# Fixed slots for a batch-wise attention stage of a four-part transformer block, with four smaller moves around it

## The chip, the cores and the metric

The kernel runs on one core of one Trainium2 chip. The metric is the device time of one execution in microseconds (us); lower is better. The core has five engines that each take their own instructions in order and wait for one another through semaphores: TensorE (PE) does matrix products and transposes, VectorE (DVE) and ScalarE (ACT) do element-wise work, GpSimd (POOL) does a few small operations and indexed transfers, and SyncE (SP) issues the other transfers between the memory of the chip (DRAM) and the core's own memory. Matrix products are accumulated in a small memory of their own (PSUM) and have to be copied out of it by DVE or ACT.

## The reference, cut to what matters

Tokens are 8 batches of 512 with 256 features, all in 32-bit floats. Four sublayers follow each other; each adds its output, times a learned scalar, to the tokens:

```python
x = x + tanh(g_xattn[0]) * gated_cross_attention(layernorm(x), ctx, boxes)   # 16 heads of 64, keys from ctx
x = x + tanh(g_ffn[0])   * ffn0(layernorm(x))
x = x + tanh(g_xattn[1]) * cross_attention(layernorm(x), ctx)                # one head of 256, then Wl on 8 copies
x = x + tanh(g_ffn[1])   * spiking_ffn(layernorm(x))                         # relu^2, then 5 steps of a neuron
```

Inside `ffn0` the attention runs across the batch, not along the sequence, and a mixture of experts with a hard capacity follows:

```python
y1 = ln(x + mha(x))             # 4 heads of 64; the 8 tokens with the same position attend to each other
gates = softmax(y1 @ wg); idx = argmax(gates)          # 8 experts
loc = number of earlier tokens with the same idx       # in the order of position, then batch
keep = loc < 512                                       # the others get nothing
y2 = ln(y1 + keep * gate * expert[idx](y1))            # 256 -> 1024 -> 256
```

The last sublayer ends in five steps per element, each with a comparison, a multiply-add and a reset:

```python
mem = 0.9 * mem + y - (mem > 1);  spikes += (mem > 1)
```

## The kernel before, in words

The kernel has five stages, one after the other.

1. `gated_cross_attention`, lines 258 to 584. A prologue goes over the 8 batches (lines 366 to 382). For each it loads the context and the tokens (`load`), makes keys, values and queries with 512-column products and stores them to DRAM (lines 221, 237 and 250), and makes small box terms (`box`, lines 137 to 158). Between batches it also loads constants for the gates (`wst`, twice 928 KB), the output weights `wo` and the box keys `kd`, and it prepares the first gate features: `offsets` on DVE, `sizes` and `log` on ACT, then `turns`, `whole`, `rest` and `rest_sizes` on DVE, `sines` on ACT, and `place`, four transfers of 520 KB. Key and query results go through a staging tile `st` with four buffers. In the prologue the order on every engine is made by the framework's scheduler. The main loop over 32 query tiles (lines 535 to 584) is written out by hand for PE, ACT and DVE and is not changed.
2. `batch_attention`, lines 591 to 763. The 4096 tokens form 32 tiles of 128 tokens (16 positions by 8 batches), in 8 groups of four. `project(g)` normalises a group, transposes it, and makes queries and keys (four 512-column pairs, `pq`) and values (`pv`). `attend(j)` takes one tile: scores for four heads (`pS`), a mask that leaves only tokens of the same position (`sm`), the row maximum (`nm`), four exponentials (`e`), their transposes (`pT`, copied to `eT` by ACT), the products with the values (`po`, scaled to `o` by DVE), two transposes (`pt2`, copied to `oT` by ACT), the output product (`pw`) and the residual (`res`). `finish(g)` normalises the group (`y1`), stores it, transposes it and makes the logits `lg`. The scheduler orders all engines. After each group `late.load(g)` fetches weights for later stages; at group 2 it also sums the 8 blocks of the matrix `WlT` into `wl` on DVE, from a staging tile with one buffer, in two loads of 1024 KB.
3. `experts`, lines 988 to 1070. `late.keys(b)` makes keys and values of the third sublayer for all 8 batches; `route` (lines 766 to 860) turns the logits into a slot for every token, a chain of small DVE steps with three products in its middle; 32 indexed transfers on POOL scatter the tokens (line 1000); then eight experts run, each on 512 tokens.
4. and 5. `tail`, lines 1076 to 1413, gathers the experts' results and does sublayers three and four for one batch after the other, in an order written by hand. Its last lines (1392 to 1413) run the two last batches: `hidden` and `drive` are products, `neurons(b, t0, t1)` is a chain of 13 DVE operations on the tiles t0 to t1 of a batch, read from `y`, which ACT copies out of PSUM.

A pool hands its memory on when it is closed, and the first instruction that writes memory of a closed pool waits for the last user of it, a store by a transfer included. In `with tc.manual_schedule(engines=...)` the engines named keep the program's own order.

Of the kernel before, what the change touches and what calls it, by code (L numbers as in the profile page):

```python
# [11 lines left out]
F32 = mybir.dt.float32  # L12
# [7 lines left out]
P = 128  # L20
# [4 lines left out]
LH = 4  # L25
# [232 lines left out]
def gated_cross_attention(cx, a, tg, x1d, d):  # L258
# [4 lines left out]
    with ExitStack() as es:  # L263
# [90 lines left out]
        with ExitStack() as pro:  # L354
            batch = project_all(cx, a, d, pro)
            bp = pro.enter_context(tc.tile_pool(name="bq", bufs=1))
            box = box_terms(cx, a, d, pro)
            bx = bp.tile([P, NSTEP * NP, 2], F32, name="bx")
            nc.sync.dma_start(out=bx, in_=a["boxq"])
            nc.sync.dma_start(out=crow, in_=a["crow"])  # L360
            nc.vector.tensor_tensor(qs, bx[:, :, 0], bx[:, :, 1], ALU.add)
            nc.vector.tensor_scalar(qs, qs, 0.5, None, ALU.mult)
            nc.vector.tensor_tensor(qi, bx[:, :, 1], bx[:, :, 0], ALU.subtract)
            nc.vector.tensor_scalar(qi, qi, 1.0, None, ALU.add)
            nc.vector.reciprocal(qi, qi)
            for b in range(B):
                batch(b)
                box(b)
                if b == 0:
                    for w in wst:  # L370
                        nc.sync.dma_start(out=w[0:GR], in_=a["wst"])
                    nc.sync.dma_start(out=wo, in_=a["woT"])
                    bo = cx.bcast(cp, a["bo"], "bo")
                    load_keys(0)
                if b in (1, 3, 5):
                    j = b // 2
                    offsets(j, 0, NP)
                    features(j, sizes, clip, log)
                if b in (2, 4):
                    j = b // 2 - 1  # L380
                    load_products(j)
                    features(j, turns, whole, rest, rest_sizes, sines, place)
# [208 lines left out]
def batch_attention(cx, a, y1, lg, x1d, y1d, between):  # L591
# [4 lines left out]
    with ExitStack() as es:  # L596
# [25 lines left out]
        yg_ = y1d.rearrange("(l g s) d -> g s l d", l=B, s=P // B)  # L622

        def load(g):
            xg = wk.tile([P, 4, D], F32, name="xg", tag="xg")
            for j in range(4):
                nc.sync.dma_start(out=xg[:, j, :], in_=xg_[4 * g + j])
            return xg

        def project(xg):  # L630
            mv, rs = cx.stats(wk, xg, 4)
            xf = wk.tile([P, 4, D], F32, name="xf", tag="xf")
            cx.normalize(xf, xg, mv, rs, 4)
            xfT = wk.tile([P, 2, 4 * P], F32, name="xfT", tag="xfT")
            for c in range(2):
                pt = ps.tile([P, 4, P], F32, name="pt", tag="t", bufs=2)
                for j in range(4):
                    nc.tensor.transpose(pt[:, j, :], xf[:, j, c * P : (c + 1) * P], ident)
                nc.scalar.copy(xfT[:, c, :], pt.rearrange("p j t -> p (j t)"))
            qkT = wk.tile([P, 4, 4 * P], F32, name="qkT", tag="qkT")  # L640
            for m in range(4):
                pq = ps.tile([P, 4 * P], F32, name="pq", tag="q", bufs=2)
                for c in range(2):
                    nc.tensor.matmul(
                        pq, wi[:, c, m * P : (m + 1) * P], xfT[:, c, :],
                        start=(c == 0), stop=(c == 1),
                    )
                nc.scalar.activation(qkT[:, m, :], pq, AF.Identity, bias=bqk[:, m : m + 1])
            v = wk.tile([P, 4, D], F32, name="v", tag="v")
            for j in range(0, 4, 2):  # L650
                pv = ps.tile([P, 2, D], F32, name="pv", tag="q", bufs=2)
                for k in range(2):
                    for c in range(2):
                        nc.tensor.matmul(
                            pv[:, k, :], xfT[:, c, (j + k) * P : (j + k + 1) * P],
# [3 lines left out]
                    v[:, j : j + 2, :], pv, bv.unsqueeze(1).to_broadcast([P, 2, D]), ALU.add  # L659
                )  # L660

            nc.vector.tensor_tensor(xf, xf, ob.unsqueeze(1).to_broadcast([P, 4, D]), ALU.add)
            return xf, qkT, v

        def attend(j, xf, qkT, v, res):

            tok = slice(j * P, (j + 1) * P)
# [15 lines left out]
            e = wk.tile([P, LH, P], F32, name="e", tag="e")  # L683
            se = wk.tile([P, LH], F32, name="se", tag="se")
            for k in range(LH):
                nc.scalar.activation(
                    e[:, k, :], smf[:, k, :], AF.Exp, bias=nm[:, k : k + 1],
                    accum_out=se[:, k : k + 1],
                )
            rec = wk.tile([P, LH], F32, name="rec", tag="rec")  # L690
            nc.vector.reciprocal(rec, se)
            pT = ps.tile([P, LH, P], F32, name="pT", tag="t", bufs=2)
            for k in range(LH):
                nc.tensor.transpose(pT[:, k, :], e[:, k, :], ident)
            eT = wk.tile([P, LH, P], F32, name="eT", tag="eT")
            nc.scalar.copy(eT, pT)
            po = ps.tile([P, LH, HD], F32, name="po", tag="o")
            for k in range(LH):
                h = 2 * (k % 2) + k // 2
                nc.tensor.matmul(  # L700
                    po[:, h, :], eT[:, k, :], v[:, j, h * HD : (h + 1) * HD],
                    start=True, stop=True,
                )
            o = wk.tile([P, LH, HD], F32, name="o", tag="o")
# [5 lines left out]
            )  # L710
            pt = ps.tile([P, 2, P], F32, name="pt2", tag="t", bufs=2)
            of = o.rearrange("p h d -> p (h d)")
            for c in range(2):
                nc.tensor.transpose(pt[:, c, :], of[:, c * P : (c + 1) * P], ident)
            oT = wk.tile([P, 2, P], F32, name="oT", tag="oT")
            nc.scalar.copy(oT, pt)
# [3 lines left out]
            nc.vector.tensor_tensor(res[:, j, :], pw, xf[:, j, :], ALU.add)  # L720

        def finish(g, res):
            mv, rs = cx.stats(wk, res, 4)
            for j in range(4):
                y = y1[:, 4 * g + j, :]
                nc.vector.scalar_tensor_tensor(
                    y, res[:, j, :], mv[:, j, 0:1], g1, ALU.subtract, ALU.mult
                )
                nc.vector.scalar_tensor_tensor(y, y, rs[:, j : j + 1], b1, ALU.mult, ALU.add)
                nc.sync.dma_start(out=yg_[4 * g + j], in_=y)  # L730
            pl = ps.tile([P, 4, NE], F32, name="pl", tag="l")
            for j in range(0, 4, 2):
                pt = ps.tile([P, 2, 2, P], F32, name="pt3", tag="t", bufs=2)
                for k in range(2):
                    for c in range(2):
                        nc.tensor.transpose(
                            pt[:, k, c, :], y1[:, 4 * g + j + k, c * P : (c + 1) * P], ident
                        )
                yT = wk.tile([P, 2, 2, P], F32, name="yT", tag="yT")
                nc.scalar.copy(yT, pt)  # L740
                for k in range(2):
                    for c in range(2):
                        nc.tensor.matmul(
                            pl[:, j + k, :], yT[:, k, c, :], wg[:, c, :],
                            start=(c == 0), stop=(c == 1),
                        )
            nc.vector.tensor_copy(lg[:, 4 * g : 4 * g + 4, :], pl)

        xgs = {0: load(0)}
        nxt = project(xgs.pop(0))  # L750
        last = None
        for g in range(NG):
            cur = nxt
            if g + 1 < NG:
                nxt = project(load(g + 1))
            res = wk.tile([P, 4, D], F32, name="res", tag="res")
            for j in range(4):
                attend(j, *cur, res)
            if last is not None:
                finish(g - 1, last)  # L760
            last = res
            between(g)
        finish(NG - 1, last)


# [110 lines left out]
class Late:  # L876
# [43 lines left out]
    def load(self, g):  # L920
# [14 lines left out]
        if g == 2:  # L935

            self.w["wl"] = wl = pool.tile([P, 2, D], F32, name="wl")
            with tc.tile_pool(name="wl8", bufs=1) as w8:
                for c in range(2):
                    wl8 = w8.tile([P, 8, D], F32, name="wl8", tag="wl8")  # L940
                    nc.sync.dma_start(out=wl8, in_=a["WlT"][:, :, c, :])
                    nc.vector.tensor_reduce(
                        wl[:, c, :], wl8.rearrange("p j d -> p d j"), AX.X, ALU.add
# [10 lines left out]
    def open(self, es):  # L954
        tc = self.cx.tc
        self.wk = es.enter_context(tc.tile_pool(name="kwk", bufs=2))
        self.ps = es.enter_context(tc.tile_pool(name="kps", bufs=2, space=PSUM))

    def keys(self, b):
        nc, w, d, wk, ps = self.cx.nc, self.w, self.d, self.wk, self.ps  # L960
        ctxT = self.ctxT.pop(b)
        for m in range(2):
            pp = ps.tile([P, S], F32, name="pp", tag="p")
# [5 lines left out]
            kT = wk.tile([P, S], F32, name="kT", tag="kT", bufs=3)  # L969
            nc.scalar.activation(kT, pp, AF.Identity, bias=w["bk"][:, m : m + 1])  # L970
            nc.sync.dma_start(out=d["ck"][b][:, m, :], in_=kT)
        for k in range(0, NQ, 2):
            pv = ps.tile([P, 2, D], F32, name="pv", tag="p")
# [6 lines left out]
            v = wk.tile([P, 2, D], F32, name="v", tag="v", bufs=3)  # L980
# [4 lines left out]
        self.context(b + self.AHEAD)  # L985


def experts(cx, a, y1, lg, late, moe, gkd, disp, yd, between):

    tc, nc, ident = cx.tc, cx.nc, cx.ident  # L990
    with ExitStack() as es:
        late.open(es)
        late.keys(0)
# [31 lines left out]
        for b in range(1, B):  # L1025
            late.keys(b)
# [49 lines left out]
def tail(cx, d, w, cp, x1, y1d, gslot, gk, yd, tg, out):  # L1076
# [5 lines left out]
    with ExitStack() as es:  # L1082
# [271 lines left out]
        with tc.manual_schedule(engines=TAIL_MANUAL):  # L1354
# [47 lines left out]
            features(("e", f + 1))  # L1402
            drive(f, 2, 2)
            drive(f, 3, 3)
            fire = neurons(f)
# [11 lines left out]
def flamingo_gated_block(ctx: ExitStack, tc: tile.TileContext, a, out):  # L1417
# [32 lines left out]
    with ExitStack() as es:  # L1450
# [12 lines left out]
        batch_attention(cx, a, y1, lg, x1d, y1d, late.load)  # L1463
# [142 lines left out]
```

## Time and profile before

| | us |
|---|---|
| median of 3 runs | 3078.8 |
| lowest and highest run | 3076.96 and 3089.75 |
| the profiled execution, its own time | 3057.43 |
| its span (first to last instruction) | 3055.6 |
| prologue (first instruction to the first gate product) | 0 to 373.4 |
| batch attention (first load of tokens to the last logits) | 1981.2 to 2279.9 |
| route and scatter (to the first expert's transposes) | 2279.9 to 2346.4 |
| experts (to the last gathers) | 2346.4 to 2584.5 |
| tail | 2584.5 to 3055.6 |

Busy time of the engines in the span: PE 2927.1 us (96%), its weight loads 2128.4, DVE 1818.9 (60%), ACT 1406.5 (46%), POOL 138.2. In rows of the profile a line such as `pw<-ow,oT 128*128 128x256 f32 x4` names the result, its inputs, the shape and how many instructions were merged; 32-bit products appear as two records each. The ends of matrix products are modelled, so a busy PE can hold gaps that only the starts of the instructions show. `[idle before <-releaser]` says how long an engine stood idle and what ended it.

### The profile page before, as it was taken

The page shows a single profiled execution, that of the slowest core. Times are in us where ns is not written, and L with a number is a line of the kernel's source. Part 1 is how long each engine was busy: PE and PEld are TensorE (multiplying, and loading weights), DVE is VectorE, ACT ScalarE, POOL GpSimd, SP SyncE. Part 2 cuts the span into 40 slices and gives each one's busy share as a digit, 9 for nine tenths or more (in the row PEclk, how much of TensorE's full clock was granted, in tenths as well). Part 3 has the DMA queues.
Part 4 walks back from the last instruction along what each step waited for, and adds up shares of the span by engine and source line. Part 5 has one row for each costly group of instructions (what it writes and reads, how often), then busy time and mean ns, then how long its engine had stood idle before and what let it go on. Part 6 is the DMA issues. An engine that isn't in the chain of part 4 may idle for free. (4 is left out here: it accounts for less than half of the span.)

```text
span 3055.6 us, 39493 instructions
## 1 busy us (share of the span) xinstructions
PE 2927.1 (96%) x15334; PEld 2128.4 (70%) x15334; DVE 1818.9 (60%) x2828; ACT 1406.5 (46%) x2196; POOL 138.2 (5%) x130
## 2 busy tenths in 40 slices
PE   7999999999999999999999999889999997799998
PEld 3444478888888888888888888756665665456566
DVE  2532276777777777777777766565542101666757
ACT  2532256656566556665656564234431111243433
POOL 1000000000000000000000000000004000221100
PEclk9999999999999999999999999999979999899999
DMA  6766565464555555555545554440016332111100
GB/s 221 223 186 189 157 193 164 130 167 132 165 135 159 139 157 142 149 157 141 156 137 156 137 161 123 119 171 28 22 49 213 134 117 105 62 42 59 32 14 21
DMA packets 275099, 394.47 MB, mean 129 GB/s; under 512 B 55456, under 2 KB 139056, under 8 KB 271736
## 3 DMA queue, kind: packets, MB, share of 16 engines
q1 hardware_dynamic: 271840, 383.54, 43.3%
q0 software_dynamic: 3072, 8.39, 0.8%
q8 instruction: 122, 2.00, 0.3%
q14 instruction: 65, 0.53, 0.1%
HBM read 237.24 MB, written 86.46 MB: 106 GB/s over the span
## 5 line engine op out<-in xcount | busy, mean ns | idle before, releaser
L451 ACT ACTIVATE e<-pS,nm 128x512 f32<-128x512 f32 x512 | 323.7, 683 | 576.4 <-DVE nm L448 576.0
L424 PE MATMUL pg<-wst,emb 116*128 116x208 f32 (+1 forms) x2560 | 581.4, 350 | 6.7 <-DVE gate L430 5.6
L424 PEld LDWEIGHTS pg<-wst,emb 116*128 116x128 f32 x2560 | 414.0, 189 | 203.2 <-issue 80.6
L480 PEld LDWEIGHTS po<-v,at 128*128 128x128 f32 x4096 | 493.0, 192 | 0.1
L480 PE MATMUL po<-v,at 128*128 128x65 f32 x4096 | 485.7, 272 | 0.0
L448 DVE TENSOR_REDUCE nm<-pS 128x2 f32<-128x1024 f32 x256 | 312.5, 1221 | 180.5 <-PE pS L444 179.3
L462 DVE SCALAR_TENSOR_TENSOR at<-gate,pT 128x1024 f32<-128x1024 f32 x256 | 311.0, 1215 | 46.7 <-PE pT L460 45.6
L444 PE MATMUL pS<-kT,qT 64*128 64x512 f32 x1024 | 291.3, 641 | 6.6 <-DMA kT<-kdr 2.9
L460 PE MATMUL pT<-ident,e 128*128 128x128 f32 x2048 | 266.4, 273 | 0.0
L460 PEld LDWEIGHTS pT<-ident,e 128*128 128x128 f32 x2048 | 239.7, 141 | 14.0 <-issue 2.3
L430 DVE COPY gate<-pg 128x416 f32<-128x416 f32 (+1 forms) x289 | 164.5, 570 | 35.0 <-PE pg L424 31.4
L430 ACT COPY gate<-pg 128x416 f32<-128x416 f32 x351 | 166.3, 530 | 34.6 <-PE pg L424 32.1
L1062 DVE TENSOR_TENSOR ye<-py,b 128x256 f32<-128x256 f32 x32 | 13.6, 424 | 210.0 <-PE py L1058 210.0
L1053 ACT ACTIVATE hT<-ph,eb 128x512 f32<-128x512 f32 x64 | 44.0, 687 | 186.0 <-PE ph L1049 186.0
L212 PE MATMUL pk<-xnT,wq 128*128 128x512 f32 x256 | 114.2, 601 | 9.8 <-ACT st L216 9.6
L62 POOL TENSOR_TENSOR ln_rs<-ln_ve,mhalf 128x4 f32<-128x4 f32 x24 | 25.0, 1042 | 2146.1 <-DMA xg<-x1d 1609.1
L212 PE MATMUL pk<-ctxT,wk__113 128*128 128x512 f32 x256 | 113.8, 601 | 7.7 <-DMA ctxT<-in_ctxT 7.7
L1265 PE MATMUL ph<-xnT,wf 128*128 128x512 f32 (+2 forms) x320 | 118.7, 513 | 1.7 <-ACT xnT L1135 1.7
L511 PE MATMUL pw<-wo,oT 128*128 128x256 f32 x512 | 115.9, 379 | 0.5 <-ACT oT L503 0.5
L1049 PE MATMUL ph<-dT,w 128*128 128x512 f32 x256 | 114.0, 604 | 2.4 <-DVE dT L1041 2.4
L227 PE MATMUL pv<-wv,ctxT 128*128 128x512 f32 x256 | 114.2, 595 | 0.0
L444 PEld LDWEIGHTS pS<-kT,qT 64*128 64x128 f32 x1024 | 77.9, 184 | 52.0 <-issue 36.3
(228 smaller groups left out, 3974.4 us busy)
## 6 DMA issues: line engine op xcount, KB each, us to landing
v<-vdr SPq DMA_DIRECT2D x256, 260.0 KB
kT<-kdr SPq DMA_DIRECT2D x256, 256.0 KB
emb<-lt SPq DMA_DIRECT2D x64, 520.0 KB
emb<-nt SPq DMA_DIRECT2D x64, 520.0 KB
vdr<-vs SPq DMA_DIRECT2D x8, 2080.0 KB
kdr<-st SPq DMA_DIRECT2D x64, 256.0 KB
qdr<-st SPq DMA_DIRECT2D x64, 256.0 KB
qT<-qdr SPq DMA_DIRECT2D x32, 512.0 KB
```

Source lines behind the costliest of these rows:

```text
L212: nc.tensor.matmul(pk, w[:, c, m * P : (m + 1) * P], src[:, c, :], start=(c == 0), stop=(c == 1))
L227: nc.tensor.matmul(pv, ctxT[:, c, kc * P : (kc + 1) * P], wv[:, c, n * 512 : (n + 1) * 512], start=(c == 0), stop=(c == 1),)
L424: nc.tensor.matmul(pg[:, c, 0 : nq * H], embs[i % 2][R, blk // 2, blk % 2, kc * P : (kc + 1) * P], wst[i % 2][R, q0 * H : (q0 + nq) * H], ...
L430: copy(gates[i][:, :, 2 * hf : 2 * hf + 2, q0 : q0 + nq].rearrange("p h k q -> p k h q"), pg[:, :, 0 : nq * H].rearrange("p k (q h) -> p k ...
L444: nc.tensor.matmul(pS[:, t, :], qTs[i][rows, p, :], kT[rows, :], start=True, stop=True)
L448: nc.vector.tensor_reduce(nm, pS, AX.X, ALU.max, negate=True)
L451: nc.scalar.activation(e[:, t, :], pS[:, t, :], AF.Exp, bias=nm[:, t : t + 1])
L460: nc.tensor.transpose(pT[:, t, kc, :], e[:, t, kc * P : (kc + 1) * P], ident)
L462: nc.vector.scalar_tensor_tensor(at, gates[i][:, 2 * p : 2 * p + 2], 1e-6, pT, ALU.max, ALU.mult)
L480: nc.tensor.matmul(po[:, 2 * (p % 2) + t, :], at[:, t, kc, :], v[:, kc, t, :], start=(kc == 0), stop=(kc == NQ - 1),)
L511: nc.tensor.matmul(pw, oT[:, c, :], wo[:, c, :], start=(c == 0), stop=(c == PAIRS - 1))
L1265: nc.tensor.matmul(ph[:, 0:n], wf[:, c, f * P : (f + 1) * P], xnT[:, c, tok], start=(c == 0), stop=(c == 1),)
```

## The change

Five things are changed.

- In the prologue SP keeps the program's own order. `load_keys(0)` comes right after batch 0; `wst` is loaded after batches 1 and 3, and `wo` and `bo` after batch 5.
- `batch_attention` is cut into small steps that are placed by hand: a slot per tile, with the projection of the next group, the norms of the group after that and the finish of the previous group spread over the four slots of a group. PE, ACT, DVE and POOL keep this order. The tile `xf` has three buffers.
- The load and sum of `WlT` is done in four pieces of 512 KB instead of two of 1024 KB, through the same single buffer. It stands in the order of DVE after the last slot of group 2.
- `late.keys` becomes a generator of four pieces. Batches 0 and 1 are done piece by piece in the drain of `batch_attention`, in its own tiles; `experts` does batches 2 to 7.
- `neurons` of the last but one batch is done in two halves; the first half follows the second of the four `drive` calls.

```diff
@@ prologue
-            for b in range(B):
-                batch(b)
-                box(b)
-                if b == 0:
-                    for w in wst:
-                        nc.sync.dma_start(out=w[0:GR], in_=a["wst"])
-                    nc.sync.dma_start(out=wo, in_=a["woT"])
-                    bo = cx.bcast(cp, a["bo"], "bo")
-                    load_keys(0)
+            with tc.manual_schedule(engines={mybir.EngineType.SP}):
+                for b in range(B):
+                    batch(b)
+                    box(b)
+                    if b == 0:
+                        load_keys(0)
+                    if b in (1, 3):
+                        nc.sync.dma_start(out=wst[b // 2][0:GR], in_=a["wst"])
+                    if b == 5:
+                        nc.sync.dma_start(out=wo, in_=a["woT"])
+                        bo = cx.bcast(cp, a["bo"], "bo")
...
@@ batch_attention: project becomes in_stats, in_norm, in_turn, qk(g, m), val(g, j), residual;
@@ attend becomes scores, turn, weigh, turn_out, mix; finish becomes out_stats, out_norm, logits_turn, logits
+        def in_norm(g):
+            if g < NG:
+                xfs[g] = wk.tile([P, 4, D], F32, name="xf", tag="xf", bufs=3)
+                cx.normalize(xfs[g], xgs.pop(g), *lns.pop(g), 4)
...
-            rec = wk.tile([P, LH], F32, name="rec", tag="rec")
-            nc.vector.reciprocal(rec, se)
+            nc.vector.reciprocal(rec, rec)
...
+        def slot(k):
+            g, j = divmod(k, 4)
+            if k:
+                turn(k - 1)
+            scores(k)
+            if k:
+                weigh(k - 1)
+            if j == 0:
+                in_stats(g + 2)
+                in_turn(g + 1)
+            elif j == 1:
+                out_stats(g - 1)
+                qk(g + 1, 1)
+                in_norm(g + 2)
+            elif j == 2:
+                out_norm(g - 1, 0, 3)
+                qk(g + 1, 3)
+            else:
+                out_norm(g - 1, 3, 4)
+                logits_turn(g - 1, 0)
+                logits_turn(g - 1, 2)
+            if k:
+                turn_out(k - 1)
+            if j == 0:
+                qk(g + 1, 0)
+            elif j == 1:
+                qk(g + 1, 2)
+            elif j == 2:
+                val(g + 1, 0)
+            else:
+                val(g + 1, 2)
+                residual(g + 1)
+            if k:
+                mix(k - 1)
+            if j == 3:
+                logits(g - 1)
+
+        def staged(name, shape):
+            if name == "p":
+                return ps.tile(shape, F32, name="pq", tag="q", bufs=2)
+            return wk.tile(shape, F32, name=name, tag="sm" if name == "kT" else "e")
+
+        load(0)
+        load(1)
+        with tc.manual_schedule(engines=MANUAL | {mybir.EngineType.Pool}):
+            in_stats(0)
+            in_norm(0)
+            in_turn(0)
+            for m in range(4):
+                qk(0, m)
+            in_stats(1)
+            val(0, 0)
+            val(0, 2)
+            residual(0)
+            in_norm(1)
+            for g in range(NG):
+                load(g + 2)
+                for j in range(4):
+                    slot(4 * g + j)
+                late.load(g)
+            g = NG - 1
+            fill = late.keys(0, staged)
+            turn(NK - 1)
+            next(fill)
+            weigh(NK - 1)
+            next(fill)
+            turn_out(NK - 1)
+            next(fill)
+            mix(NK - 1)
+            out_stats(g)
+            next(fill, None)
+            fill = late.keys(1, staged)
+            next(fill)
+            out_norm(g, 0, 2)
+            logits_turn(g, 0)
+            next(fill)
+            out_norm(g, 2, 4)
+            logits_turn(g, 2)
+            next(fill)
+            logits(g)
+            next(fill, None)
...
@@ Late.load, g == 2
-                for c in range(2):
-                    wl8 = w8.tile([P, 8, D], F32, name="wl8", tag="wl8")
-                    nc.sync.dma_start(out=wl8, in_=a["WlT"][:, :, c, :])
+                for k in range(4):
+                    c, cols = k // 2, slice(k % 2 * P, k % 2 * P + P)
+                    wl8 = w8.tile([P, 8, P], F32, name="wl8", tag="wl8")
+                    nc.sync.dma_start(out=wl8, in_=a["WlT"][:, :, c, cols])
                     nc.vector.tensor_reduce(
-                        wl[:, c, :], wl8.rearrange("p j d -> p d j"), AX.X, ALU.add
+                        wl[:, c, cols], wl8.rearrange("p j d -> p d j"), AX.X, ALU.add
                     )
...
@@ experts
-        for b in range(1, B):
-            late.keys(b)
+        for b in range(2, B):
+            for _ in late.keys(b, staged):
+                pass
...
@@ end of tail
             drive(f, 1, 1)
             features(("e", f + 1))
+            some(neurons(f, 0, 2), NT)
             drive(f, 2, 2)
             drive(f, 3, 3)
-            fire = neurons(f)
+            fire = neurons(f, 2, NQ)
```

## The prediction

> **What bounds the kernel now.** I read the page first: PE's share, the 40 slices, the granted clock.
>
> ```profile
> PE 2927.1 (96%) x15334; PEld 2128.4 (70%) x15334; DVE 1818.9 (60%) x2828; ACT 1406.5 (46%) x2196; POOL 138.2 (5%) x130
> ...
> PE   7999999999999999999999999889999997799998
> ...
> PEclk9999999999999999999999999999979999899999
> ```
>
> PE is the bound nearly everywhere; the change touches its weak slices: the first (prologue), 26 to 30 (76 us each: batch attention, route, scatter) and the last. Next the windows, cut where a group's last DVE copy of logits, `lg`, ends the group (start, length, busy time of PE, PEld, DVE, ACT, POOL, then granted clock, DMA share, GB/s).
>
> ```profile
> 2111.30:2146.00 34.70, 31.77 (x170) 21.88 (x170) 19.83 (x55) 15.00 (x48) 2.11 (x2) 0.95 0.11 31
> 2213.50:2246.50 33.00, 30.96 (x173) 22.09 (x173) 19.31 (x47) 16.18 (x54) 2.21 (x2) 1.00 0.06 17
> 2246.50:2279.90 33.40, 28.05 (x116) 23.36 (x115) 11.21 (x33) 7.98 (x24) 1.11 (x1) 0.55 0.11 32
> ```
>
> A group takes 33 us at full clock. PE's 31 "busy" hold gaps: by starts of instructions (128x256 0.216 us a record, 128x512 0.429, transposes 0.109, `po` 0.12, `pl` 0.107) its work is 25.9 us a group. No engine is full, so chains set the period. The timeline of one tile shows the chain (start, length, idle before):
>
> ```profile
> 2227.99 0.42 DVE L705 TENSOR_TENSOR o<-po,rec 128x256 f32<-128x256 f32 x1 [1.58 <-PE po L700]
> ...
> 2228.47 0.44 PE L714 MATMUL pt<-ident,o 128*128 128x128 f32 x2 [0.52 <-DVE o L705]
> ...
> 2228.61 0.66 DVE L676 TENSOR_TENSOR sm<-pS,mask 128x512 f32<-128x512 f32 x1
> ...
> 2229.30 0.69 DVE L682 TENSOR_REDUCE nm<-sm 128x4 f32<-128x512 f32 x1
> ...
> 2229.43 0.58 ACT L696 COPY eT<-pT 128x512 f32<-128x512 f32 x1
> 2229.92 0.40 ACT L686 ACTIVATE e<-sm,nm 128x128 f32<-128x128 f32 x1
> ```
>
> PE waits for DVE and ACT in turn; ACT's four exponentials start 1.3 us after the mask and occupy it for 1.6.
>
> **The change part by part.**
>
> *Slots.* Per group the work stays 25.9 us of PE; DVE sums to about 22.7, ACT to 15.5. I laid the written order out slot by slot with the durations above. PE's work: 3.02 us in every slot (turn 0.44, scores 0.52, weigh 0.97, turn_out 0.22, mix 0.87), plus 2.59, 3.44, 3.45, 4.31 in slots 0 to 3. Waits: each slot about 0.42 for `eT` (copy 0.58 after the transposes, less the scores that cover it). In slots 0 and 3 a second one: turn_out needs a transposes' buffer (two exist) that holds the projection's or the logits' transposes; their ACT copies stand behind the four exponentials, which wait for `sm` and `nm` (0.69 each). That costs about 2.0 us in slot 0 and 1.8 in slot 3. With what DVE adds: 7.85, 6.93, 6.94, 9.58, so 31.3 us a group; group 0, without a finish, 29.3, group 1 31.8, group 7, which projects nothing, 25.6. Slot 0 should start at about 2003.4 (`pv` of group 0 today 1999.9, and its 3.6). Groups 0 to 6 then need 217.5: 2220.9; group 7 ends at 2246.5. The gain on the 33 to 35 of today is only about 2 to 3 a group.
>
> *The sum of `WlT`* is today in the start of the stage:
>
> ```profile
> L942 DVE TENSOR_REDUCE wl<-wl x2: 3691/3692/3694, 2001.4 to 2011.5; 128x256 f32<-128x2048 f32 x2
> ...
>   DMA wl<-in_WlT: 7.4, 2
> ```
>
> Its second 1 MB load goes out at 2005.1, after the first reduce has freed the one buffer, and the second reduce starts at 2011.5: 6.35 us. Now the built kernel's order has four reduces in a row on DVE after slot 11. Each has half the data, 1.85 us; only the first load can be early, the other three are each issued after the reduce before. Behind them on DVE stand `sm`, `nm` and `o` of slot 12: ACT's exponentials and then PE wait. The load of 512 KB is not in the trace. If all of 6.35 is size, it takes 3.2; if all is fixed, 6.35. The Trainium skill, "DMA: Bandwidth & Descriptors", section "Anatomy of one DMA — SWDGE (gpsimd) path", gives a transfer about 2.0 us fixed and the rest by bytes (its fit is for the gpsimd path, these go through SP): estimate 2.0 + 4.35/2 = 4.2. It speaks against cutting a serial load in pieces: by bytes alone DVE stands 1.85 + 3 x 5.05 = 17.0, by the page 20.0, all fixed 26.4. I take 20, of which PE is covered for the first 0.3: +19.7. What the two old reduces cost in the startup is already off: slot 0 starts right behind the first values. SP's own queue loses nothing by its waits there: the loads behind are for later stages.
>
> *Clock.* The last window above has no PE gap over about 1.3 us, yet 0.55. The Trainium skill, "TensorE: Matmul & The Clock Gate", "Part 1: The HAM clock gate", tells of half rate after an idle window of about 3.4 us. By that alone only the 20 us stop would lower the clock (+2 after it). The row disagrees, and decides: thin PE work also lowers it. Slots 0 and 3 and group 7 (no projection) are such. I add 2 at the start, 2 after the sum, 3 at the boundaries between slots 3 and 0, and in group 7 the 10 by which its 25.6 grow at half clock, since the row shows just that group at 0.55: 17, between 0 and 26. Slots end at 2246.5 + 19.7 + 17 = 2283.2.
>
> *Drain and keys 0, 1.* Two batches of keys are 14 us of PE beside the last tile and the norm: last `lg` 20 us after the slots, 2303. Route's first operation in addition takes over memory of the closed stage, and so waits for the store of the last values piece: route starts 25 after, at 2308.2 (today 2280.2). Inside route `pc` stood behind a batch of keys:
>
> ```profile
> 2285.45 0.62 DVE L819 TENSOR_REDUCE hs<-hot 128x8 f32<-128x256 f32 x1
> ...
> 2289.06 0.59 PE L815 MATMUL pc<-hot,order 128*128 128x256 f32 x2
> ...
> 2297.46 1.19 POOL L1000 DMA_INDIRECT disp<-y,slot  x1 [17.10 <-DVE sl L855]
> ```
>
> I give 1.5 of it back: 15.7 instead of 17.2. First scatter 2323.9 against 2297.5: **+26.4**. What follows does not shorten: 32 scatters at 1.27 us reach 2338 today, the experts' transposes 2346.4. The keys lay beside them (PE 41.5 busy of 48.9 in that window), so moving two batches ahead frees PE where POOL sets the end, and puts 14 us on the path before it.
>
> *Prologue.* The loads of `wst` and `wo` sit ahead of the stores that free `st`:
>
> ```profile
> 57.57 1.35 ACT L216 ACTIVATE st<-pk,bq 128x512 f32<-128x512 f32 x2 [11.76 <-DMA qdr<-st]
> ...
> 58.31 4.21 PE L212 MATMUL pk<-xnT,wq 128*128 128x512 f32 x5 [9.62 <-ACT st L216]
> ```
>
> With 1.9 of half clock it is 11.5; a stall of 2.7 stays in batch 0 (values' store of 2 MB), so -8.8. But with SP in program order, `place` (2.08 MB) and the loads stand before the key stores of batches 3 and 5, and the built order puts ACT's feature steps in the middle of those batches' key copies, behind DVE's `offsets`: about 5 us of PE each. Elsewhere in the prologue PE is unbroken. Net **+1**, between -8 and +7. `load_keys(0)`, moved up, is read only in the main loop: nothing.
>
> *Neurons.* In the tail's end DVE is the chain, 16.7 us of 128x1024 and four quarters of 5.93:
>
> ```profile
> 3012.48 0.69 DVE L1295 TENSOR_SCALAR cnt<-y 128x1024 f32<-128x1024 f32 x1 [12.01 <-ACT y L1284]
> ...
> 3029.21 0.30 DVE L1295 TENSOR_SCALAR cnt<-y 128x256 f32<-128x256 f32 x1
> ...
> 3041.17 0.37 ACT L1284 COPY y<-py 128x256 f32<-128x256 f32 x1 [2.83 <-PE py L1280]
> ```
>
> The first half's `y` is there at 3004.7, in 12 us of idle DVE; a half is about 9.5 us, so the second ends at 3023.8. The quarters then follow their own `y` (3022.8, 3026.3, 3033.9, 3041.5): the end moves from 3052.8 to 3047.5, **-5.3**.
>
> *Smaller edits:* the third `xf` buffer and the reciprocal in place add no instruction; POOL's `ln_rs` (1.1 us) in fixed order starts a slot or more ahead of its reader. Nothing, as long as that slot lies between.
>
> *Sum:* 1 + 26.4 - 5.3 = +22. The profiled execution's 3057.4 (span 3055.6) becomes 3079.5. The median of the runs is 21 above that execution; I add the 22 to it: 3078.8 + 22 = **3101**.
>
> **The rivals.**
> - *Slots pack.* If the transposes' buffers come free in time (exponentials early, copies ahead), only the `eT` wait is left: 25.9 + 4 x 0.42 = 27.6 a group, 26 less over seven; and PE so dense holds its clock as in the window at 1.00, 3 less at the boundaries and 10 in group 7. 22 - 39 = -17: 3062. This is the other side, by one mechanism: in slots 0 and 3 the ACT copies are not held by the exponentials. It turns the sign below 30.0 us a group if the clock comes along ((22 - 13)/7 under my 31.3), below 28.2 if not. For it: ACT is busy 16 of 33, DVE 19. Against: the order puts the copies behind.
> - *Clock stays up.* Same slots, clock term 2 instead of 17, the sum in 17 instead of 20: +4, 3083. For it: the window at 1.00 has as many gaps.
> - *The drain hides keys.* Keys fill PE's gaps in the last tile and route's wait for the store is short, 7 less: +15, 3094.
> - *Everything late.* Prologue +7 for +1, the sum's loads all fixed (+6.4), clock at its upper end (+9): +43, 3122. For it: the 0.55 row, and SP's order.
>
> **How the numbers follow.** A measurement here can tell about 0.5%, 15.4 us, from no change. Forecast 0.50, of which a fifth lies under +15.4; late 0.14; clock up 0.09; drain 0.08, half on each side of the bound; packed 0.19, of which 0.15 beyond -15.4. Slower 0.40 + 0.14 + 0.04 = 0.58; same 0.10 + 0.09 + 0.04 + 0.04 = 0.27; faster 0.15. The range, 3060 to 3120, leaves out the fast end of the packed case (the prologue's -8 on top) and the last of the late one. The likeliest case by itself is 3090 to 3112: clock 7 either way, the sum's load 3.
>
> **What would show it.** Right: the `lg` copies 31 to 32 us apart; one DVE stop of about 20 us near 2100 with four 1.85 us reduces; PE idle in slots 0 and 3 released by ACT's transposes' copies; `mx` waiting for a store of `v`; first scatter near 2324; in the prologue the 9.6 us gone, and waits in batches 3 and 5; first half of `neurons` from about 3004 of today's scale. Wrong: a period below 29, the sum done in the shadow of other work, clock 1.00 in group 7, or a tail that keeps its 3052.8 minus the start's shift.

## The result, and the profile after

The changed kernel takes 3120.3 us (median of 4 runs, 3117.5 to 3124.7) against 3082.8 for the kernel before: 1.0122 times as long, 95% interval 1.0094 to 1.015. The direction was forecast, +22; the measured +37.5 puts the kernel just above the range, whose upper end was 3120.

The kernel before takes about 3059 us on one chip and 3080 to 3084 on another, here called the first and the second chip, so every comparison below is made with runs of the kernel before on the same chip. On which chip the runs of this section were made is not recorded; by their times they are like the second (the profile before, 3057.4, is like the first). The page of the kernel after, its PE busy time, and the slices of PE and of its granted clock:

```profile
PE 2928.7 (94%) x15334; PEld 2129.1 (68%) x15334; DVE 1827.7 (59%) x2844; ACT 1403.9 (45%) x2196; POOL 139.6 (4%) x130
...
PE   8898999999999999999999999886885999599998
...
PEclk9999999999999999999999999998987999899999
```

PE's work is that of before (2927.1), its share is lower: time was added, not work. Slices 2 and 4 (prologue) and the slices of batch attention and scatter have new dents. The windows from one `lg` copy to the next, which hold the slots of groups 2, 3, 4 and 7 (start, length, PE, PEld, DVE, ACT, POOL, clock, DMA share, GB/s):

```profile
2097.30:2128.40 31.10, 27.67 (x171) 20.62 (x168) 21.42 (x57) 14.62 (x48) 2.19 (x2) 1.00 0.12 35
2128.40:2180.50 52.10, 29.19 (x170) 21.32 (x168) 28.29 (x58) 14.61 (x48) 2.19 (x2) 0.80 0.17 51
2180.50:2213.30 32.80, 29.37 (x171) 21.85 (x169) 21.02 (x55) 14.61 (x48) 2.19 (x2) 0.95 0.06 16
...
2275.50:2307.40 31.90, 25.28 (x129) 20.06 (x128) 15.10 (x40) 11.03 (x42) 1.01 (x1) 0.71 0.06 17
```

A steady group takes 31.1 us, and one of them 52.1. The lines of the sum of `WlT` say why that one:

```profile
L1063 DVE TENSOR_REDUCE wl<-wl x4: 1871/1872/1902, 2128.3 to 2147.0; 128x128 f32<-128x1024 f32 x4
...
  DMA wl<-in_WlT: 13.1, 3
```

Three waits of 4.4 us and four reduces of 1.87: DVE is taken for 20.6 us in a row. The start of route, from the instructions that use `lg`: its maximum over the experts, `mx`, comes 6.7 us after the last `lg` (2336.0 after 2329.3), and 4.4 of that is the wait for a store of the keys' last piece.

```profile
L910 DVE TENSOR_REDUCE mx<-lg x1: 422/422/422, 2336.0 to 2336.0; 128x32 f32<-128x256 f32 x1
...
  DMA cvd<-v: 4.4, 1
```

The prologue at the change from batch 1 to batch 2, from the timeline:

```profile
105.42 0.51 SPq L373 DMA_DIRECT2D wst<-in_wst  x1
106.02 0.35 SPq L173 DMA_DIRECT2D ctxT<-in_ctxT  x1
106.42 0.43 SPq L175 DMA_DIRECT2D xt<-in_x  x1
...
126.51 0.75 DVE L59 BATCH_NORM_STATS2 ln_st<-xt 128x6 f32<-128x256 f32 x2 [12.45 <-DMA xt<-in_x]
127.23 1.31 ACT L216 ACTIVATE st<-pk,bk 128x512 f32<-128x512 f32 x2 [18.27 <-DMA kdr<-st]
...
127.97 2.07 PE L212 MATMUL pk<-ctxT,wk__113 128*128 128x512 f32 x2 [12.06 <-ACT st L216]
```

Right behind the moved load of `wst`, the load of `xt` needs 20 us and a key store as long; ACT has no free `st`, PE stands for 12 us. The same follows the second load, at batch 4, where PE stands for 7.3 us. The first gate product starts at 400.9 instead of 373.4. Further down, the last scatter and the first expert:

```profile
2389.91 0.96 POOL L1124 DMA_INDIRECT disp<-y,slot  x1 [0.30 <-issue]
...
2419.38 0.69 DVE L1166 COPY dT<-pt 128x512 f32<-128x512 f32 x1 [5.79 <-PE pt L1163]
```

The copy of the first expert's transposes, `dT`, begins 29.5 us after the start of the last scatter. And the end of the tail, the first DVE step of each part of the neurons, halves and then quarters:

```profile
3074.28 0.43 DVE L1420 TENSOR_SCALAR cnt<-y 128x512 f32<-128x512 f32 x1 [4.23 <-ACT y L1409]
...
3083.82 0.43 DVE L1420 TENSOR_SCALAR cnt<-y 128x512 f32<-128x512 f32 x1
...
3093.35 0.29 DVE L1420 TENSOR_SCALAR cnt<-y 128x256 f32<-128x256 f32 x1
```

A half is 9.5 us, and the first fills what was 12 us of idle DVE.

### The profile page after: what moved, and what is told of

The parts are those of the page before. It is cut to its first block, busy times and chain, and to the rows that moved or that the text cites. A ratio compares the mean times of both kernels' runs of the same rounds, so it can differ in the third digit from the quotient of the medians.

```text
span 3120.1 us, 39511 instructions
## 1 busy us (share of the span) xinstructions
PE 2928.7 (94%) x15334; PEld 2129.1 (68%) x15334; DVE 1827.7 (59%) x2844; ACT 1403.9 (45%) x2196; POOL 139.6 (4%) x130
## 5 line engine op out<-in xcount | busy, mean ns | idle before, releaser
L231 DVE TENSOR_TENSOR vs<-pv,bv 128x512 f32<-128x512 f32 x64 | 43.9, 688 | 148.8 <-PE pv L227 148.6
L212 PEld LDWEIGHTS pk<-ctxT,wk__113 128*128 128x128 f32 x256 | 50.0, 199 | 94.9 <-issue 67.2
```

What stands on the lines that cost most here:

```text
L212: nc.tensor.matmul(pk, w[:, c, m * P : (m + 1) * P], src[:, c, :], start=(c == 0), stop=(c == 1))
```

## The experiments

**The kernel before, on two chips.** No edit.

> The kernel before, unchanged. Its four runs shown lie 20 to 33 us above its profiled execution (3057.4). Theory A: the excess is one place, a wait of some 20 us that an execution has or has not, and the place is the scatter, where the kernel after has one transfer share in sixteen late and 18.9 us between the last scatter and the first expert that the profile of before does not have; then this profile shows about 28 us there instead of 9.6 whenever its span is near 3077. Theory B: the excess is spread as a lower granted clock over the main loop; then the scatter is as in the first profile and the stages are longer by 0.6% each.

> The kernel before once more. Its runs lie near 3059 on one chip and near 3083 on another. Theory A: the 24 us are one place, the end of the keys beside the scatter: where the runs are near 3083, the stretch from the last scatter to the first expert's transposes is about 33 us instead of 9, since the stores of keys and values land late while the scatters run. Theory B: spread over the stages, 0.8% each. If this chip is of the 3059 kind, the profile is as the first.

The first came out at 3056.8, 0.9997 times the other runs of that kernel (0.9985 to 1.0008), with a profile like the first one shown: the chip was of the 3059 kind, so it could not tell. The second came out at 3084.3, with a span of 3083.5. Against the profile of the first chip, its route starts 2.9 us later and its experts 30. The windows while the scatters run, and from there to the experts, first on the first chip, then on the second:

```profile
2298.00:2338.00 40.00, 38.37 (x131) 24.31 (x130) 7.44 (x11) 7.96 (x12) 30.55 (x32) 1.00 0.93 328
2338.00:2347.00 9.00, 3.74 (x18) 3.08 (x17) 1.38 (x2) 0.29 (x1) 0.20 (x1) 0.94 0.67 238
```

```profile
2301.00:2341.00 40.00, 26.04 (x71) 15.56 (x70) 3.54 (x6) 4.12 (x6) 30.49 (x32) 0.81 0.62 232
2341.00:2377.00 36.00, 25.23 (x77) 15.42 (x77) 5.44 (x8) 4.12 (x6) 0.54 (x1) 0.78 0.47 165
```

POOL needs the same 40 us for its 32 scatters. Beside them 328 GB/s move on the first chip and 232 on the second, where PE does little more than half of the keys' products, and the rest follows: 36 us instead of 9. Theory A holds as to the place: of the 34 us between these two profiles 27 lie between the first scatter and the experts. Which transfer is the slow one is only in part shown (there ACT waits 14 us for a load of `ctxT`, while the profile doesn't name what the longest waits of DVE, 31 us, are for), and why these transfers are slower there is not known.

**Neurons in halves alone.** To the kernel before:

```diff
             features(("e", f + 1))
+            some(neurons(f, 0, 2), NT)
             drive(f, 2, 2)
             drive(f, 3, 3)
-            fire = neurons(f)
+            fire = neurons(f, 2, NQ)
```

> The kernel before with the last but one neurons in two halves and nothing else. The forecast of this part alone is -5.3 us against the kernel before, at the end of the tail: last store of x some 5.3 us earlier after the first gather of the tail; the profile after shows 6.1 less from gather to end. Rival: the first half on DVE delays ACT's and PE's work of the last batch, then 0.

3052.7 against 3058.9: 0.9978 (0.9969 to 0.9988), -6.2 us. The forecast's -5.3 lies in the interval, the rival's 0 does not.

**The old prologue in the kernel after.** Edit: the loop over batches as before, without SP's fixed order.

> The kernel after with the prologue of the kernel before. If the prologue is worth what the two profiles show (first gate product 400.9 against 373.4), this is 27 us faster than the kernel after, 3093. If the forecast of +1 for it was right for most executions and the profile after was an odd one, it is within 5 us of 3120.

3071.8 on the first chip, 1.0041 times the kernel before (1.0029 to 1.0053), first gate product at 374.5. The rest of the change thus costs +12.9 us there. The kernel after itself was not run on the first chip, so the 27 us that were expected can't be read as a difference of two times; the gate product shows them, 374.5 against 400.9.

**The weights' loads cut at row 112.**

```diff
-                        nc.sync.dma_start(out=wst[b // 2][0:GR], in_=a["wst"])
+                        nc.sync.dma_start(out=wst[b // 2][0:112], in_=a["wst"][0:112])
+                        nc.sync.dma_start(out=wst[b // 2][112:GR], in_=a["wst"][112:GR])
```

> The kernel after with each load of the gates' weights cut into rows 0 to 111 and rows 112 to 115. Theory A: the 116-row load goes to four of the sixteen DMA engines, since behind it every transfer has twelve shares that land early and four that land 9 to 12 us late; 112 rows go to sixteen, so the waits of 12.7 us behind batch 1 and of 7.9 behind batch 3 go to under 3 each: first gate product at 380 to 386, 15 to 20 us faster than the kernel after. Theory B: what counts is the bytes ahead of the key stores (928 KB) in the order of SP; then nothing changes, first gate product at 400.

3074.9 on the first chip, 1.0051 (1.0031 to 1.0071). The first gate product starts at 376.5, 24.4 us earlier than in the kernel after, with the same bytes at the same places in the same order of SP. Theory B is out, and the gain is above the 15 to 20 that theory A gave. The windows behind the first load, in the kernel after and then with the cut:

```profile
115.00:120.00 5.00, 0.91 (x3) 0.08 (x1) 0.00 (x0) 0.00 (x0) 0.00 (x0) 0.79 0.41 139
120.00:125.00 5.00, 0.00 (x0) 0.00 (x0) 0.00 (x0) 0.00 (x0) 0.00 (x0) 0.50 0.20 70
```

```profile
115.00:120.00 5.00, 5.00 (x13) 2.23 (x12) 3.78 (x14) 0.79 (x2) 1.01 (x1) 1.00 0.29 109
120.00:125.00 5.00, 5.00 (x13) 2.09 (x12) 1.63 (x3) 0.69 (x1) 0.00 (x0) 1.00 0.27 101
```

In the kernel after every engine stands from about 116 on, and the sixteen DMA engines are busy to 0.20, as much as three of them at work; the others have nothing to do. With the cut PE is busy throughout. The Trainium skill, "DMA: Bandwidth & Descriptors", section "Why a DMA increments its semaphore by 16 and not by 1", has the rule: a transfer runs on the largest number of engines up to 16 that divides its outer dimension. 116 rows (4 x 29) give 4, 112 give 16, and a transfer counts as landed only when its last share has. So four engines carry 928 KB alone, and each later transfer of sixteen shares has four behind that. The traces agree: counted from their DMA packets, the 116 rows of 8 KB took 16.8 us in the kernel after with 3.3 of them under way on average, and 4.2 us with 13.3 under way after the cut.

**The kernel after and the cut once more, on the second chip.**

> The kernel after, unchanged, beside the other three of this group. Its first profile had 28.5 us between the last scatter and the first expert's transposes, the kernels with an other prologue had 6.4. Theory A (a part of the change makes it): again about 28. Theory B (chance of one execution, one share of each store late by 10 to 25 us): 6 to 10 this time, and the whole about 3098, which is the 3074.9 of the run with cut weight loads plus the 24.4 that its first gate product is earlier. Prologue in both theories: first gate product near 400.

> The kernel after with cut weight loads, again, as the common base of this group. Where before is near 3059: +16. Where before is near 3083: +12 to +16, because two batches of keys fewer (7 us each) lie behind the scatter there, less the 24 that their place in the drain costs.

The kernel after: 3116.3, 1.0114 (1.0095 to 1.0133), first gate product at 399.0, and 25.5 us from the last scatter's end to the copy `dT`. It was not chance (B), but not the change either (A): the kernel before has 35.9 us there on this chip (9.1 on the first), and the kernel with the cut 27.6 (6.4 on the first), so that the chip makes it. With the cut, in another series of runs on that chip: 3098.5, 1.0056 (1.0039 to 1.0072), +18.3, a little over what was expected; so the loads as they stand cost 18 us by the medians (15 when each kernel is taken against the kernel before of its own series), 21 by the first gate product (399.0 and 378.3). This 3098.5 is the base of the next three experiments; they ran in the other series on the same chip, with the kernel before at 3083.0 there and at 3080.1 here, so that their differences from the base are uncertain by some 3 us.

**The sum of `WlT` spread over four slots** (with the cut). Its pieces become a generator that issues a load before slot 8 and, after each of the slots 8 to 11, reduces and issues the next:

```diff
+                if g == 2:
+                    sums = late.sums()
+                    next(sums)
                 for j in range(4):
                     slot(4 * g + j)
+                    if g == 2:
+                        next(sums, None)
```

> The kernel after with cut weight loads (rows 0 to 111 and 112 to 115), and the four pieces of the sum of WlT after slots 8, 9, 10 and 11 instead of all four after slot 11; each load has a slot of 7 us to land and is there when its reduce of 1.87 us comes. The forecast's theory (serial loads stop DVE for 20 us, the data of one load need only 4.4): group 2 falls from 52 us to 31 plus 4 x 1.87 that fall partly into idle DVE, 31 to 38; 14 to 21 us faster than the run with cut loads alone, 3054 to 3061. Rival (the stop is in the shadow of something that comes late anyway): no more than 5 us.

3079.8 on the second chip, 18.7 under the base's 3098.5, 0.9991 of the kernel before (0.9981 to 1.0000). The absolute figure that was expected was worked out for the first chip, where this kernel was not run; the difference is as forecast (14 to 21). The line of the reduces, with nothing under its heading of waits:

```profile
L1079 DVE TENSOR_REDUCE wl<-wl x4: 1898/1907/1912, 2082.8 to 2109.5; 128x128 f32<-128x1024 f32 x4
```

**ACT's copies ahead of the exponentials in slots 0 and 3** (with the cut). The exponentials become a step of their own, called after `scores` in slots 1 and 2, and after `turn_out` in slots 0 and 3.

```diff
             scores(k)
+            if j in (1, 2):
+                exps(k)
...
                 turn_out(k - 1)
+            if j in (0, 3):
+                exps(k)
```

> The kernel after with cut weight loads; in slots 0 and 3 of each group ACT does the copies xfT, or yT, and oT first and the four exponentials behind them, PE and DVE as before. The forecast's theory (turn_out waits for a transposes' buffer whose copy stands behind the exponentials, 2.0 and 1.8 us): a group falls from 31.1 to 27 to 28, 20 to 28 us less over seven groups, about 3050. Rival (the exponentials are then late for the next slot's turn, the wait moves to slots 1 and 0): 31 us a group stays, within 4 us of 3075.

3080.0 on the second chip, 18.4 under the base: the theory's way, but less than the 20 to 28 that it gave. A group takes 29.1 instead of 31.1, not 27 to 28:

```profile
2176.30:2205.40 29.10, 27.44 (x170) 20.65 (x168) 21.00 (x54) 14.53 (x48) 2.19 (x2) 1.00 0.07 20
```

From one `eT` copy to the next, slot 0 fell from 7.83 to 6.36, slot 3 only from 9.57 to 9.05. In slot 3 PE waits for something else, as the timeline of the kernel after on this chip shows:

```profile
2179.53 0.20 PEld L746 LDWEIGHTS pt<-ident,o 128*128 128x128 f32 x2 [1.89 <-ACT xfT L653]
...
2200.37 0.44 PE L783 MATMUL pt<-ident,y 128*128 128x128 f32 x2 [1.19 <-DVE y L774]
2201.05 0.44 PE L746 MATMUL pt<-ident,o 128*128 128x128 f32 x2 [0.24 <-ACT yT L787]
```

The first line is slot 0, the weight load of turn_out's transpose: it waits 1.9 us for the copy `xfT`, and with ACT's order changed 0.5 us of that wait is left. The second is slot 3: the logits' transposes wait for `y`, which `out_norm` finishes in the same slot; behind it only 0.24 is left of the wait that was forecast.

**All keys beside the scatter** (with the cut). Edit: no `late.keys` in the drain; `experts` takes batches 0 to 7.

> The kernel after with cut weight loads, and all eight batches of keys beside the scatter again, none in the drain of the batch attention. The forecast's theory (two batches of keys put 14 us of PE and the wait for a store of 4.4 on the path before route; beside the scatter POOL sets the end): route starts 12 to 18 us earlier after the last slot, 8 to 15 of it are left at the first expert. Rival (keys 0 and 1 then end after the last scatter): two batches at 7 us come back behind the scatter, within 4 us of 3075.

3103.3 on the second chip, 1.0072 (1.0054 to 1.0089), 4.9 over the base, and 2 over it when each is taken against the kernel before of its own series. Route starts 11.6 us earlier after the stage's start (315.3 instead of 326.9), but from the first scatter to the experts it takes 82.5 instead of 68.1: 14.4 come back. The windows while the scatters run, and from there to the experts:

```profile
2314.40:2354.80 40.40, 20.54 (x48) 11.07 (x48) 2.77 (x5) 2.75 (x4) 30.95 (x32) 0.73 0.60 225
2354.80:2397.00 42.20, 33.79 (x110) 22.65 (x111) 7.07 (x11) 6.18 (x9) 0.03 (x1) 0.86 0.52 187
```

The forecast's theory fell on this chip; the rival was right. Whether it holds on the first chip, where the stores keep up, was not tried.

**Together.** Cut, spread, copies ahead, and all of `out_norm` in slot 2:

```diff
-                out_norm(g - 1, 0, 3)
+                out_norm(g - 1, 0, 4)
...
-                out_norm(g - 1, 3, 4)
```

> The kernel after with cut weight loads, the sum of WlT spread over the slots of group 2, ACT's copies ahead of the exponentials in slots 0 and 3, and all of out_norm in slot 2 (slot 3 then need not wait for y). If the gains add: 18 for the sum, 14 for the copies, up to 1 a group more for out_norm: 32 to 38 under the base, and 16 to 24 under the kernel before. Rival: the spread reduces and out_norm in slot 2 make DVE late there, 4 us a group: then 8 to 15 less of it.

3057.6 on the second chip: 0.9924 of the kernel before (0.9904 to 0.9945), 22.5 us faster, and 40.9 under the base, more than the 32 to 38 that were expected. A group takes 28.2 us, two of them 29.4; slot 3 takes 8.1. The slots of groups 6 and 7:

```profile
2184.20:2212.40 28.20, 27.50 (x171) 20.68 (x169) 17.41 (x42) 14.53 (x48) 1.01 (x1) 1.00 0.07 19
2212.40:2241.80 29.40, 24.34 (x130) 19.17 (x129) 15.01 (x39) 11.19 (x42) 1.01 (x1) 0.71 0.07 19
```

> As the one before it in this group, and all eight batches of keys beside the scatter. Where before is near 3059, stores land in time and the forecast's theory says: route 15 us earlier, 8 to 15 of it kept: faster than the other by 8 to 15. Where before is near 3083, two batches come back behind the scatter: slower than the other by 0 to 8.

3063.8, 0.9938 (0.9921 to 0.9954): 6.2 over the other by the medians, the second case that was expected, though the two intervals overlap. In the profiles the first scatter to the experts takes 83.3 instead of 68.5.

## Why the prediction was right or wrong

The stages of the kernel after against the kernel before, from the two profiles of the second chip, beside the forecast (the 30.8 between the two profiles stand for 33.3 between the medians there, and for 37.5 in the first comparison):

| | forecast | measured |
|---|---|---|
| prologue, to the first gate product | +1 | +25.1 (399.0, 373.9) |
| main loop | 0 | -0.5 (1606.2, 1606.7) |
| batch attention and drain, to `mx` | +28 | +22.9 (325.7, 302.8) |
| route | -1.5 | -3.2 (14.4, 17.6) |
| first scatter to the copy of the experts' first transposes | 0 | -10.6 (65.9, 76.5) |
| experts | 0 | +1.2 (237.1, 235.9) |
| tail | -5.3 | -4.1 (466.0, 470.1) |
| sum | +22 | +30.8 (spans 3114.3, 3083.5) |

**Prologue: wrong, the step that failed.** The forecast took the old stall off and put 5 us of PE each on batches 3 and 5, but gave the moved loads of `wst` no price at their new places, ahead of the stores of batches 2 and 4, beyond being part of what stands before the key stores. It counted bytes; what counted was that a load of 116 rows runs on four engines and makes all that is issued behind it late. That cost 12.1 and 7.3 us of PE in the first profile (8.2 and 7.4 in the second), and a lower clock behind each wait (0.64 from 128 to 133 us in the first), where one wait of 9.6 had been. The rest of the step was about right: with the cut, the new prologue is 2.5 us longer than the old one (376.5 and 374.0 on the first chip), and the forecast was +1. In batches 3 and 5 PE then waits 3.1 and 4.6 us, mostly for DVE's copy `tT` of the box terms, which the forecast did not name. Without the failed step, that is with the cut, the whole change costs +16.0 on the first chip and +18.3 on the second, where +22 was forecast.

**Slots: right.** Forecast 7.85, 6.93, 6.94, 9.58 and 31.3 a group; measured 7.83, 6.84, 6.86, 9.57 and 31.1. In slot 0 the wait was what the forecast said (2.0 forecast, 1.5 taken away by the experiment). In slot 3 the size was right by luck, for the cause was mostly wrong: `y` was late, not `yT`.

**Sum of `WlT`: right.** Forecast 4.2 us a load by the page and +19.7; measured 4.4 and 21.0 (52.1 less 31.1), and 18.7 came back when the loads were given a slot each.

**Clock: somewhat too much.** Counted from the first load of tokens to `mx`, the forecast is 310 us without its clock term and 327 with the 17. Measured are 326.1 in the first profile of the kernel after and 323.8 in that of the second chip, so 14 to 16 are left for the term, and not all of that is clock. The steady groups ran at 1.00; one or two groups of each profile took 1.7 longer at 0.95, in their slot 3 and not right behind the sum. Group 7 took 31.9 and 33.6 at 0.71 and 0.65, where 25.6 and 10 on top were forecast; that the clock makes all of the excess was not tested. From there to `mx` it took 28.5 and 27.5 instead of 25. The stage of the kernel before is also 1.5 longer on the second chip, and so the change costs 5 less in this stage than forecast.

**"What follows does not shorten": wrong on the second chip.** The forecast read from one profile that the keys are hidden beside the scatter. There, they are not: 36 us of waiting and keys follow the last scatter, and with two batches fewer the stretch is 10.6 shorter. This and the 5 us in batch attention took back 16 of the 24 us that the prologue cost over the forecast; that the sum ended so near the range is luck.

**Tail: right**, -5.3 against -4.1 in the profiles and -6.2 by itself.

**The sum against the median: the warning was there.** The profiled execution lay 21 us under the median of the runs. The forecast added the 21 as if it were spread. By the two chips measured later, most of it is one stage that differs from chip to chip, and a stage in which the change moved work.

## What to carry to other kernels

Look at the outer dimension of a transfer before you move it: 116 rows ahead of the stores of a pipelined stage cost 15 to 24 us here, and with 112 plus 4 that cost was gone. A serial chain of load and reduce through one buffer belongs into slots with a load ahead, not into one place behind a fixed order. When the profiled execution and the runs differ by more than the noise, find the stage before you cost a change to it.

## What the runs showed of the hardware that was not expected

- Two chips differ by 21 to 28 us in this kernel, most of it in one stage: while the indexed transfers run with other transfers beside them, 328 GB/s move on one and 232 on the other.
- The granted clock fell to 0.71 in group 7 with PE busy for 25 of 32 us, and was 1.00 in groups with PE busy for 27.7 of 31.1. The longest gap of PE does not explain it: 1.1 us in group 7, 1.6 in the steady group ahead of it.
- The kernel before against itself on the second chip gave 1.0015 (1.0004 to 1.0026), so a difference of 0.15% between two kernels is not told by such runs.
